# Two graph attention layers on one core: three PSUM banks for the lists' sums and a division one list later, one bank in turn for a closing's projections

## The chip, the cores and the metric

The kernel runs on one core of a Trainium2 chip. The metric is the device time of one execution in microseconds (us), from the runs shown below; lower is better. PE is the matmul engine, DVE the vector engine, ACT the scalar engine, POOL the general engine that issues the gathers here, and SP the engine that issues most other transfers. PE writes its results to PSUM[...]; DVE and ACT read them from there.

## The reference

Two layers over the same graph of 4096 nodes, whose adjacency is about 0.8% full and symmetric, with features of width 256. In each layer every node takes a softmax-weighted mean over its neighbours, adds its input and is normalised.

```python
def _gat(x, adj, W_heads, a1, a2, W_out, b_out):      # layer 0: 8 heads of 128
    Wh = jnp.einsum('nf,hfd->hnd', x, W_heads)
    s1 = jnp.einsum('hnd,hd->hn', Wh, a1)
    s2 = jnp.einsum('hnd,hd->hn', Wh, a2)
    e = s1[:, :, None] + s2[:, None, :]
    e = jnp.where(e > 0, e, ALPHA * e)
    e = jnp.where(adj[None, :, :] > 0, e, NEG)
    att = jax.nn.softmax(e, axis=-1)
    hp = jax.nn.elu(jnp.einsum('hnm,hmd->hnd', att, Wh))
    feat = jnp.transpose(hp, (1, 0, 2)).reshape(N, NHEADS * NHID)
    return feat @ W_out + b_out
...
x = _layernorm(x + _L0_gnn_ref(x, adj, ...), axis=-1)
x = _layernorm(x + _L1_gnn_ref(x, L1_gnn_W, L1_gnn_a, adj), axis=-1)   # layer 1: 4 heads of 64
```

## The kernel before

The two layers are done in different ways. The second is dense: all 4096 x 4096 weights are formed by DVE and multiplied by PE; it begins at about 1828 us of the profile, and the change touches none of it. The first is sparse, and everything that follows is about it.

**Lists.** The 4096 nodes are cut into 256 lists of 16 nodes (`T`), eight lists to a block of 128 nodes (`GT`), 32 lists to a phase (`GP`). For each list a selection on DVE has written the numbers of all neighbours outside the own block. POOL gathers the rows of these neighbours (features and score factors) into `G`, four gathers of 128 rows (L917), five lists ahead. DVE then forms the weights `e` of the list in `weigh` (a copy of the factors, three operations of 128x512 and a bit test; L1022 to L1037), for 8 heads times 16 nodes. `gathered` (L1040) sums rows times weights on PE in one PSUM bank, `po`: one matmul for the block's own rows (`own`), one for rows shared by four lists (`Gs`), four for `G`. Each fp32 matmul leaves two records in the profile, so a list has 12. Column 256 of `po` is the sum of the weights. `invert` (L1062) takes its reciprocal on DVE, `divide` (L1067) scales the sums on ACT into `ag`, which frees the bank, and `flip` (L1072) turns `ag` on PE (`pa`) and copies it on ACT into `aT`.

**The order.** Nothing reorders these instructions: each engine gets them in the order in which the loop at L1253 to L1321 writes them, and works them off in that order, waiting where it must. One pass of that loop (a turn, n) writes: the gathers of list n+5; `invert` and `divide` of list n - SOON; `flip` of list n - SOON - 1; `weigh` and `gathered` of list n; now and then the preparation of the next block's own rows (`Near`) and shared rows (`Shared`); a piece of counting the words for a later phase (`counts`, from turn 4 of a phase: a mask `mb` on ACT, two matmuls `pw` on PE, and twice a phase a copy `ws` on ACT, L613); some pieces of a later phase's selection on DVE (`pick`); and one piece of a closing (`late.some(1)`). SOON is 2.

**Closings.** When the eight lists of a block i are turned, `close0` (L1084) queues eight pieces, one for each of the next turns. They apply the head weights (`heads`, PE, L1105, in two halves of four heads, tiles `ph`), the ELU (`below` on ACT, L1115 and L1116, into `el`; `elu` on DVE, L1119, into `hT`) and the output projection (`project`, PE, L1126 and L1128, tile `py`). What needs the result comes with the pieces of the next closing, through the dictionary `st0["due"]`, ahead of that closing's own work in the same piece: `add` (DVE, L1134; reads `py`) in piece 0, and after every second block `spread`, `norm` and `flip` of two blocks (PE `pz`, ACT `x1T_sb`) in pieces 1 and 5 to 7.

```python
pieces = [
    [lambda: heads(0, 0)],
    [lambda: heads(0, 1)],
    [lambda: below(0), lambda: heads(1, 0)],
    [lambda: elu(0), lambda: heads(1, 1)],
    [lambda: below(1), lambda: project(0)],
    [lambda: elu(1), load],
    [lambda: project(1)],
    [],
]
```

**Second layer's scores.** When a quarter of the blocks is through (eight), `Scores.chunk` (L371) forms the second layer's scores for it in six steps (`scores` on PE into `ps`, `pull`, `top`, `factors`, `turn`, `store`), and `Projected.step` (L878) its projections; both go through `st0["then"]` and `st0["later"]` into the pieces of later closings. The same class forms the first layer's scores at the start (`opening`).

**PSUM.** Two banks serve all short transposes (`ps_m`), one holds DVE's small tables (`side`). Five belong to the pool `ps_0`: two with the tag `o0` for `po`, two with the tag `o1` for `ph`, `py` and `ps`, one with the tag `o2` for the words (`pw`, L600). A tile with one tag takes the tag's banks in turn, and its first writer waits until the last reader of what lay there is through.

Of the kernel before, what the change touches and what calls it, by code (L numbers as in the profile page):

```python
# [9 lines left out]
F32 = mybir.dt.float32  # L10
# [8 lines left out]
P = 128  # L19
# [243 lines left out]
def fast_path(  # L263
# [12 lines left out]
    N, F = x.shape  # L276
    D0, H0, _ = a0.shape
    D1, H1, _ = a1.shape
# [30 lines left out]
    ps_0 = first.enter_context(tc.tile_pool(name="ps_0", bufs=2, space=PSUM))  # L309
# [26 lines left out]
    class Scores:  # L336
# [29 lines left out]
        def chunk(self, k, src):  # L366

            n, H = self.n, self.H
            held = {}
            HC = CH // 2  # L370
            TH = HC // P  # L371

            def scores():
                ps = held["ps"] = ps_0.tile([P, HC], F32, tag="o1", name=f"ps_{n}_{k}")
                for c in range(KC):
                    for q in range(P // DQ):
                        a, half = divmod(q, 2)
                        nc.tensor.matmul(
                            ps[ts(q, DQ), :],
                            self.v[:, c, a, :],  # L380
                            src[:, c, ts(2 * k + half, HC)],
                            start=(c == 0),
                            stop=(c == KC - 1),
                            tile_position=(0, q * DQ),
                            skip_group_check=True,
                        )
# [652 lines left out]

    def gathered(n, G, e, own, shared):  # L1040

        po = ps_0.tile([P, F + 1], F32, tag="o0", name=f"po_0_{n}")

        def mul(w, v, first=False, **kw):
            nc.tensor.matmul(  # L1045
                po, w.rearrange("p h t -> p (h t)"), v[:, 0 : F + 1], start=first, **kw
            )

        mul(own.e[:, n % GT], own.rows, True, stop=False)
        a = ts(n % SL, SP)  # L1050
        mul(
            shared.e[a],
            shared.G[a],
            stop=False,
            tile_position=(n % SL * SP, 0),
            skip_group_check=True,
        )
        for b in range(NB):
            mul(e[:, b], G[:, b], stop=(b == NB - 1))
        return po  # L1060
# [21 lines left out]
    st0 = {}  # L1082

    def close0(i, aT):  # L1084


        hT = two.tile([P, H0, P], F32, tag="hT", name=f"hT_{i}", bufs=1)
        els, phs, pys = {}, {}, []
        if i % NY == 0:
            st0["mv"] = small.tile([P, NY, 2], F32, tag="mv0", name=f"mv0_{i}", bufs=2)  # L1090
            st0["rs"] = small.tile([P, NY], F32, tag="rs0", name=f"rs0_{i}", bufs=2)
            st0["ys"] = []
        mv, rs, ys = st0["mv"], st0["rs"], st0["ys"]

        def load():
            ys.append(two.tile([P, F], F32, tag="y", name=f"y_{i}", bufs=3))
            nc.sync.dma_start(ys[-1], x[ts(i, P), :])

        def heads(k, half):
            if half == 0:  # L1100
                phs[k] = ps_0.tile([P, 4, P], F32, tag="o1", name=f"ph_{i}_{k}")
            for hh in (2 * half, 2 * half + 1):
                h = 4 * k + hh
                for c in range(KC):
                    nc.tensor.matmul(  # L1105
                        phs[k][:, hh, :],
                        w_sb[:, c, ts(h, D0)],
                        aT[:, c, h, :],
                        start=(c == 0),
                        stop=(c == KC - 1),  # L1110
                    )

        def below(k):
            el = els[k] = two.tile([P, 4, P], F32, tag="el", name=f"el_{i}_{k}", bufs=1)
            nc.scalar.activation(el, phs[k], AF.Relu, scale=-1.0)  # L1115
            nc.scalar.activation(el, el, AF.Exp, scale=-1.0)  # L1116

        def elu(k):
            nc.vector.scalar_tensor_tensor(  # L1119
                hT[:, ts(k, 4), :], els[k], -1.0, phs[k], ALU.add, ALU.max  # L1120
            )

        def project(k):
            if k == 0:
                pys.append(ps_0.tile([P, F], F32, tag="o1", name=f"py_{i}"))
                nc.tensor.matmul(pys[0], ones[0:1, :], b_sb, start=True, stop=False)  # L1126
            for h in range(4 * k, 4 * k + 4):
                nc.tensor.matmul(  # L1128
                    pys[0], hT[:, h, :], wo_sb[:, h, :], start=False, stop=(h == H0 - 1)
                )  # L1130

        def add():
            y = ys[i % NY]
            nc.vector.tensor_tensor(y, y, pys[0], ALU.add)  # L1134
            st = small.tile([P, nc.vector.BN_STATS_DIM], F32, tag="st", name=f"st_0_{i}")
            nc.vector.bn_stats(st, y)
            nc.vector.bn_aggr(mv[:, i % NY, :], st)

        def spread():
            nc.vector.tensor_scalar(rs, mv[:, :, 1], EPS, None, ALU.add)  # L1140
            nc.gpsimd.tensor_tensor(rs, rs, neg_half.to_broadcast([P, NY]), ALU.pow)

        def norm(k):
            y = ys[k]
            nc.vector.tensor_scalar(
                y, y, mv[:, k, 0:1], rs[:, k : k + 1], ALU.subtract, ALU.mult
            )

        def flip(k):
            if not x1T:  # L1150
                x1T.append(big.tile([P, KC, N], F32, tag="xT", name="x1T_sb"))
            ii, y = i - NY + 1 + k, ys[k]
            nc.sync.dma_start(x1_d[ii], y)
            pz = ps_m.tile([P, KC, P], F32, tag="m", name=f"pz_{ii}")
            for cc in range(KC):
                nc.tensor.transpose(pz[:, cc, :], y[:, ts(cc, P)], ident)
            nc.scalar.copy(x1T[0][:, :, ts(ii, P)], pz)
            q = ii // CT
            turned[q] += 1
            if turned[q] == CT:  # L1160
                fs = sc1.chunk(q, x1T[0])
                m0 = q * CT
                steps = [lambda m=m: pair[0].step(m) for m in (m0, m0 + 4)]
                st0.setdefault("due", {}).setdefault(7, []).append(fs[0])
                st0["then"] = {k + 1: [f] for k, f in enumerate(fs[1:] + steps)}
                if q < NCH - 1:
                    st0["later"] = {
                        2 + k: [lambda m=m0 + 4 * k: pair[1].step(m, True)] for k in range(2)
                    }

        due = st0.pop("due", {})
        pieces = [
            [lambda: heads(0, 0)],
            [lambda: heads(0, 1)],
            [lambda: below(0), lambda: heads(1, 0)],
            [lambda: elu(0), lambda: heads(1, 1)],
            [lambda: below(1), lambda: project(0)],
            [lambda: elu(1), load],
            [lambda: project(1)],
            [],  # L1180
        ]
        for k, fs in due.items():
            pieces[k] = fs + pieces[k]
        late.add(*(lambda fs=fs: [f() for f in fs] for fs in pieces))
        due = st0["due"] = st0.pop("then", {})
        if "later" in st0 and due:
            st0["then"] = st0.pop("later")
        due.setdefault(0, []).append(add)
        if i % NY == NY - 1:
            for k, f in (  # L1190
                (1, spread),
                (5, lambda: norm(0)),
                (6, lambda: flip(0)),
                (6, lambda: norm(1)),
                (7, lambda: flip(1)),
            ):
                due.setdefault(k, []).append(f)
# [7 lines left out]
    pair = [Projected(g, wpool) for g in range(H1 // 2)]  # L1205
# [2 lines left out]

    NG = NT * GT
    AHEAD = 5  # L1210
    SOON = 2
    EXTRA = 2.5
    FIRST = 3.0
    COUNT = 4
# [23 lines left out]
    with tc.manual_schedule():  # L1238
# [13 lines left out]
        firsts.some(EARLY)  # L1252
        for n in range(NG + SOON + 1):  # L1253
            i, o, s = n // GT, n % GP, n // GP
            busy = 0.0
            if n < NG:
# [21 lines left out]
                if n % 4 == 2 and 2 <= n // 4 < 2 + NCH:  # L1278
                    inputs(1, n // 4 - 2)
            if SOON <= n < NG + SOON:  # L1280
                po, to = sums.pop(n - SOON)
                invert(n - SOON, po)
                means[n - SOON] = (divide(n - SOON, po), to)
            if n > SOON:
                ag, done = means.pop(n - SOON - 1)
                flip(n - SOON - 1, ag, done)
            if n < NG:
# [3 lines left out]
                m = n // SL + 1  # L1291
# [28 lines left out]
            if n > SOON and (n - SOON - 1) % GT == GT - 1:  # L1320
                close0((n - SOON - 1) // GT, done)  # L1321
    late.all()
    while "due" in st0 or "then" in st0:
        due = st0.pop("due", None) or st0.pop("then")
        for k in sorted(due):
            for f in due[k]:
                f()
# [186 lines left out]
    for g in range(G):  # L1514
        wh = pair[g].wh
        for c in range(NCH):
            po = open1(g, c)
# [8 lines left out]
            for j in range(NT):  # L1526
                if g + c == 0 and j % CT == CT - 2:
                    k = ts(j // CT, CT)
# [96 lines left out]
```

## Time and profile before

| | us |
|---|---|
| median of 3 runs | 2520.47 (2519.27 to 2523.54) |
| profiled execution, its own time | 2532.02 |
| its span, first to last instruction | 2530.2 |
| PE busy | 2133.9 |
| DVE busy | 1967.2 |
| ACT busy | 872.1 |
| POOL busy | 1083.4 |
| sums over lists, `G` rows (L1045), matmul busy | 623.4 (2048 records) |
| heads `ph` (L1105), matmul busy | 152.4 (1024 records) |
| projections `py` (L1128), matmul busy | 128.4 (512 records) |

The rows name a line, an engine, an operation and the tiles it writes and reads (out<-in). A wait of an engine is given with the instruction that waited, then `<-` and the instruction that ended the wait. "remote" (in the chain of waits: another core or an unknown queue) stands where the profile has no instruction for the semaphore that ended it; some matmul records are missing from the trace. The ends of matmuls are modelled. An fp32 matmul leaves two records, so 2048 records are 1024 matmuls.

### The profile page before, as it was taken

The numbers are of one execution on the slowest core, as the hardware profiler recorded it, in microseconds if no ns is written. First come the engines' busy times: TensorE is split into PE (matmuls) and PEld (weight loads), VectorE is DVE, ScalarE is ACT, GpSimd is POOL, SyncE is SP. The second block draws the span as 40 slices with busy tenths as digits, with TensorE's granted clock in tenths as the row PEclk, the third lists the DMA queues.
The fourth block names the chain that finished last, engine by engine and source line by source line (L and its number), as shares of the span: only waits on it lengthen the run. The fifth ranks groups of instructions, "written<-read, shape, count | busy, mean of one in ns | idle before, by whom it ended". The sixth has DMA issues, their size and how long they took to land.

```text
span 2530.2 us, 35637 instructions
## 1 busy us (share of the span) xinstructions
PE 2133.9 (84%) x12481; PEld 1217.2 (48%) x12481; DVE 1967.2 (78%) x4121; ACT 872.1 (34%) x1822; POOL 1083.4 (43%) x1154
## 2 busy tenths in 40 slices
PE   4377787888888887888887878878999999999997
PEld 2155455555556555555655655655643333333332
DVE  6478677787767878877786877666599999999997
ACT  1323323323323322332332222222344444455663
POOL 1455566566655666666566666656100000000000
PEclk9578888889878899888888889988999999999998
DMA  9777657456535746655564644444396666666763
GB/s 303 234 180 218 179 160 203 131 157 180 177 103 148 232 121 159 192 167 136 169 188 112 147 124 119 120 125 118 121 318 207 210 201 210 214 217 223 228 205 106
DMA packets 185796, 446.70 MB, mean 177 GB/s; under 512 B 60899, under 2 KB 92646, under 8 KB 185606
## 3 DMA queue, kind: packets, MB, share of 16 engines
q1 hardware_dynamic: 127462, 269.14, 33.8%
q0 software_dynamic: 52224, 169.97, 24.7%
q10 hardware_dynamic: 5920, 5.21, 0.6%
q8 instruction: 101, 1.65, 0.3%
q14 instruction: 89, 0.73, 0.1%
HBM read 427.62 MB, written 24.97 MB: 179 GB/s over the span
## 4 chain that ended last, share of the span: by engine, by line
PE 66%; another core or an unknown queue 13%; DVE 8%; ACT 7%; issue 4%; DMA 2%; POOL 0%; ACTq 0%; DVEq 0%; POOLq 0%; SPq 0%
PE po L1045 27%; PE po L1371 18%; PE po L1383 9%; PE py L1128 3%; PE ph L1105 3%; PE pa L1076 2%; ACT ag L1069 1%; ACT mb L588 1%; ACT rb_s L944 1%; PE pw L600 1%; DVE e L1023 1%; DVE e L1029 1%; PE pw L883 1%; DMA Ga<-in_adj 1%
## 5 line engine op out<-in xcount | busy, mean ns | idle before, releaser
L917 POOL DMA_INDIRECT G<-table,ids x1024 | 984.8, 962 | 610.9 <-issue 256.2
L1537 DVE SCALAR_TENSOR_TENSOR e<-rb,pj,mb 128x1024 f32<-128x1024 f32 x512 | 635.2, 1282 | 37.4 <-PE po L1383 13.3
L1045 PE MATMUL po<-G,e 128*128 128x257 f32 x2048 | 623.4, 456 | 17.8 <-DVE e L1037 7.7
L1371 PE MATMUL po<-e,wh 128*32 128x512 f32 x4096 | 531.3, 593 | 0.1
L1045 PEld LDWEIGHTS po<-G,e 128*128 128x128 f32 x2048 | 435.6, 224 | 186.3 <-issue 60.2
L1079 ACT COPY aT<-pa 128x256 f32<-128x256 f32 x256 | 95.3, 372 | 873.2 <-remote 267.0
L1045 PE MATMUL po<-own,eo 128*128 128x257 f32 x512 | 188.9, 454 | 237.6 <-ACT ag L1069 181.6
L1353 ACT ACTIVATE mb<-aq 128x1024 bf16<-128x1024 int32 x256 | 270.7, 1061 | 307.1 <-DVE e L1537 271.7
L1383 PE MATMUL po<-e,cj 128*32 128x512 f32 x2048 | 333.3, 592 | 0.0
L1371 PEld LDWEIGHTS po<-e,wh 128*32 128x32 f32 x4096 | 151.7, 110 | 289.7 <-issue 280.5
L1455 POOL TENSOR_SCALAR nm<-nm 128x4 f32<-128x4 f32 x6 | 5.5, 912 | 617.8 <-ACT ju L1454 617.8
L1064 DVE TENSOR_SCALAR rd_all<-po 128x1 f32<-128x1 f32 x256 | 38.7, 151 | 229.5 <-PE po L1045 153.0
L1045 PEld LDWEIGHTS po<-own,eo 128*128 128x128 f32 x512 | 86.9, 213 | 268.8 <-ACT ag L1069 202.4
L1045 PE MATMUL po<-Gs,e_s 32*128 32x257 f32 x512 | 202.7, 479 | 5.6 <-issue 5.6
L1023 DVE TENSOR_TENSOR e<-rb,side 128x512 f32<-128x512 f32 x256 | 176.0, 688 | 9.2 <-issue 0.2
L1029 DVE TENSOR_TENSOR e<-e,side 128x512 f32<-128x512 f32 x256 | 175.7, 686 | 8.8
L1037 DVE TENSOR_TENSOR e<-e,side 128x512 f32<-128x512 f32 x256 | 175.7, 686 | 8.8
L1105 PE MATMUL ph<-aT,w_sb 128*128 128x128 f32 x1024 | 152.4, 294 | 13.8 <-DVE hT L1119 6.7
L1383 PEld LDWEIGHTS po<-e,cj 128*32 128x32 f32 x2048 | 85.4, 110 | 149.0 <-issue 148.9
L1105 PEld LDWEIGHTS ph<-aT,w_sb 128*128 128x128 f32 x1024 | 140.7, 206 | 29.6 <-issue 16.5
L1069 ACT ACTIVATE ag<-po,rd_all 128x256 f32<-128x256 f32 x256 | 120.9, 472 | 70.4 <-DVE rd_all L1065 39.7
L1045 PEld LDWEIGHTS po<-Gs,e_s 32*128 32x128 f32 x512 | 84.7, 206 | 105.5 <-issue 105.4
(174 smaller groups left out, 2080.5 us busy)
## 6 DMA issues: line engine op xcount, KB each, us to landing
aq<-in_adjT SPq DMA_DIRECT2D x256, 512.0 KB
aq<-in_adj SPq DMA_DIRECT2D x108, 512.0 KB
rb<-r_d SPq DMA_DIRECT2D x48, 512.0 KB
G<-table,ids POOLq DMA_INDIRECT x1024
table<-in_x SPq DMA_DIRECT2D x8, 1024.0 KB
Ga<-in_adj SPq DMA_DIRECT2D x12, 512.0 KB
table<-tail SPq DMA_DIRECT2D x56, 98.0 KB
own<-table SPq DMA_DIRECT2D x32, 152.5 KB
```

Source lines behind the costliest of these rows:

```text
L917: nc.gpsimd.indirect_dma_start(out=G[:, b, :], out_offset=None, in_=table[s % 2][:, :], in_offset=bass.IndirectOffsetOnAxis(ap=lists[s][:, ...
L1023: nc.vector.tensor_tensor(e, rb[:, :, ts(n % GT, T)].unsqueeze(1).to_broadcast(sh), f_p[:, :, 0:H0].unsqueeze(3).to_broadcast(sh), ALU.mult,)
L1029: nc.vector.tensor_tensor(e, e, f_p[:, :, H0:].unsqueeze(3).to_broadcast(sh), ALU.max)
L1037: nc.vector.tensor_tensor(e, e, nb_p.unsqueeze(2).to_broadcast(sh), ALU.mult)
L1045: nc.tensor.matmul(po, w.rearrange("p h t -> p (h t)"), v[:, 0 : F + 1], start=first, **kw)
L1069: nc.scalar.activation(ag, po[:, 0:F], AF.Copy, scale=rd_all[:, n : n + 1])
L1079: nc.scalar.copy(aT[:, :, :, ts(n % GT, T)], pt)
L1105: nc.tensor.matmul(phs[k][:, hh, :], w_sb[:, c, ts(h, D0)], aT[:, c, h, :], start=(c == 0), stop=(c == KC - 1),)
L1353: nc.scalar.activation(mb, aq, AF.Relu, scale=OPEN)
L1371: nc.tensor.matmul(po[q][ts(b, DQ), :], wh[:, j, k, d : d + DQ], es[k][:, ts(q, HB)], start=(j == 0), stop=(j == NT - 1), tile_position=(0 ...
L1383: nc.tensor.matmul(po[NQ][r0 : r0 + DQ, :], sc1.cj[:, j, 2 * g + k : 2 * g + k + 1].to_broadcast([P, DQ]), es[k][:, ts(q, HB)], start=(j = ...
L1537: nc.vector.scalar_tensor_tensor(e, rb[k], sc1.pj[:, j, h : h + 1], mb, ALU.max, ALU.min)
```

## The change

The sums `po` get three banks (`o0`), and `SOON` becomes 3: list n - 3 is inverted and divided in turn n, list n - 4 is flipped. `ph` and `py` share one bank (`o1`), so that the halves of the heads and the projection of one closing lie there one after the other. The pieces of a closing are set anew: `heads(1, 0)` follows `elu(0)` in one piece, `project(0)` follows `elu(1)`, and the last piece, empty before, holds `project(1)`. The second layer's scores move to the words' bank (`o2`); the first layer's alternate between `o1` and `o2`. The steps of a quarter go through a list `st0["next"]` of two dictionaries: the six score steps in pieces 2 to 7 of one closing, the two or four projection steps in pieces 1 to 4 of the next.

```diff
--- before.py
+++ after.py
@@ -371,7 +371,10 @@
             TH = HC // P
 
             def scores():
-                ps = held["ps"] = ps_0.tile([P, HC], F32, tag="o1", name=f"ps_{n}_{k}")
+
+
+                tag = "o1" if n == 0 and k % 2 == 0 else "o2"
+                ps = held["ps"] = ps_0.tile([P, HC], F32, tag=tag, name=f"ps_{n}_{k}", bufs=1)
                 for c in range(KC):
                     for q in range(P // DQ):
                         a, half = divmod(q, 2)
@@ -1039,7 +1042,7 @@
 
     def gathered(n, G, e, own, shared):
 
-        po = ps_0.tile([P, F + 1], F32, tag="o0", name=f"po_0_{n}")
+        po = ps_0.tile([P, F + 1], F32, tag="o0", name=f"po_0_{n}", bufs=3)
 
         def mul(w, v, first=False, **kw):
             nc.tensor.matmul(
@@ -1098,7 +1101,7 @@
 
         def heads(k, half):
             if half == 0:
-                phs[k] = ps_0.tile([P, 4, P], F32, tag="o1", name=f"ph_{i}_{k}")
+                phs[k] = ps_0.tile([P, 4, P], F32, tag="o1", name=f"ph_{i}_{k}", bufs=1)
             for hh in (2 * half, 2 * half + 1):
                 h = 4 * k + hh
                 for c in range(KC):
@@ -1122,7 +1125,7 @@
 
         def project(k):
             if k == 0:
-                pys.append(ps_0.tile([P, F], F32, tag="o1", name=f"py_{i}"))
+                pys.append(ps_0.tile([P, F], F32, tag="o1", name=f"py_{i}", bufs=1))
                 nc.tensor.matmul(pys[0], ones[0:1, :], b_sb, start=True, stop=False)
             for h in range(4 * k, 4 * k + 4):
                 nc.tensor.matmul(
@@ -1161,30 +1164,29 @@
                 fs = sc1.chunk(q, x1T[0])
                 m0 = q * CT
                 steps = [lambda m=m: pair[0].step(m) for m in (m0, m0 + 4)]
-                st0.setdefault("due", {}).setdefault(7, []).append(fs[0])
-                st0["then"] = {k + 1: [f] for k, f in enumerate(fs[1:] + steps)}
+
                 if q < NCH - 1:
-                    st0["later"] = {
-                        2 + k: [lambda m=m0 + 4 * k: pair[1].step(m, True)] for k in range(2)
-                    }
+                    steps += [lambda m=m: pair[1].step(m, True) for m in (m0, m0 + 4)]
+                st0["next"] = [
+                    {k + 2: [f] for k, f in enumerate(fs)},
+                    {k + 1: [f] for k, f in enumerate(steps)},
+                ]
 
         due = st0.pop("due", {})
         pieces = [
             [lambda: heads(0, 0)],
             [lambda: heads(0, 1)],
-            [lambda: below(0), lambda: heads(1, 0)],
-            [lambda: elu(0), lambda: heads(1, 1)],
-            [lambda: below(1), lambda: project(0)],
-            [lambda: elu(1), load],
+            [lambda: below(0)],
+            [lambda: elu(0), lambda: heads(1, 0)],
+            [lambda: heads(1, 1)],
+            [lambda: below(1), load],
+            [lambda: elu(1), lambda: project(0)],
             [lambda: project(1)],
-            [],
         ]
         for k, fs in due.items():
             pieces[k] = fs + pieces[k]
         late.add(*(lambda fs=fs: [f() for f in fs] for fs in pieces))
-        due = st0["due"] = st0.pop("then", {})
-        if "later" in st0 and due:
-            st0["then"] = st0.pop("later")
+        due = st0["due"] = st0["next"].pop(0) if st0.get("next") else {}
         due.setdefault(0, []).append(add)
         if i % NY == NY - 1:
             for k, f in (
@@ -1208,7 +1210,7 @@
 
     NG = NT * GT
     AHEAD = 5
-    SOON = 2
+    SOON = 3
     EXTRA = 2.5
     FIRST = 3.0
     COUNT = 4
@@ -1320,8 +1322,7 @@
             if n > SOON and (n - SOON - 1) % GT == GT - 1:
                 close0((n - SOON - 1) // GT, done)
     late.all()
-    while "due" in st0 or "then" in st0:
-        due = st0.pop("due", None) or st0.pop("then")
+    for due in iter(lambda: st0.pop("due", None) or (st0.get("next") or [None]).pop(0), None):
         for k in sorted(due):
             for f in due[k]:
                 f()
```

## The prediction

> **What bounds the kernel now.** I read first the stage table (busy time in stretches), since 1,840 of the 2,530 us belong to the lists and the change touches nothing after them.
>
> ```profile
> core 0: us, PE busy (x) PEld busy (x) DVE busy (x) ACT busy (x) POOL busy (x), PEclk, DMA share, GB/s
> ...
> 800.00:1000.00 200.00, 164.59 (x727) 113.55 (x726) 155.31 (x419) 64.66 (x154) 127.45 (x133) 0.90 0.61 173
> ...
> 1840.00:2530.00 690.00, 672.14 (x6182) 218.20 (x6174) 641.21 (x568) 335.18 (x531) 18.27 (x26) 0.99 0.65 212
> ```
>
> In a stretch of lists PE has work for 82% and DVE for 78%: neither is full, so the time lies in waits. PE's own waits between 200 and 1800 us come next (total, times, longest), then DVE's and ACT's of the same stretch.
>
> ```profile
> PE po L1045 <- ACT ag L1069: 173.7, 63, 8.6
> PE po L1045 <- issue: 25.7, 28, 5.7
> PE po L1045 <- ACT lst L751: 13.6, 5, 5.6
> ...
> PE po L1045 <- DVE e L1037: 5.4, 7, 0.9
> ```
>
> ```profile
> DVE rd_all L1064 <- PE po L1045: 141.2, 70, 5.3
> DVE rd_all L1064 <- remote: 39.4, 18, 4.7
> ...
> DVE hT L1119 <- ACT el L1116: 31.8, 10, 7.1
> ```
>
> ```profile
> ACT aT L1079 <- remote: 257.8, 33, 12.4
> ACT aT L1079 <- PE pa L1076: 244.1, 68, 7.9
> ...
> ACT ag L1069 <- DVE rd_all L1065: 37.1, 22, 5.0
> ```
>
> At first sight this asks for the change: PE waits 173.7 us for `ag`, the division that frees a bank of sums, and almost never (5.4 us) for the weights `e`. DVE stands 181 us before its inverse, for PE. But who keeps `ag` waiting? The timeline of one such wait answers:
>
> ```profile
> 1067.04 0.27 PE L1076 MATMUL pa<-ident,ag 128*128 128x128 f32 x1 [0.26 <-issue]
> ...
> 1070.63 0.37 ACT L1079 COPY aT<-pa 128x256 f32<-128x256 f32 x1 [8.69 <-remote]
> ...
> 1070.90 1.15 ACT L588 ACTIVATE mb<-aq,half 128x1024 bf16<-128x1024 int32 x1
> ...
> 1071.95 0.68 ACT L613 ACTIVATE ws<-pw,half 128x512 f32<-128x512 f32 x1
> ...
> 1072.53 0.47 ACT L1069 ACTIVATE ag<-po,rd_all 128x256 f32<-128x256 f32 x1
> ...
> 1073.05 1.23 PE L1045 MATMUL po<-own,eo 128*128 128x257 f32 x2 [5.75 <-ACT ag L1069]
> ```
>
> ACT stands 8.69 us before the copy of a transposed mean, which waits for PE; then copy, mask, words and `ag` follow without a gap, and PE starts 0.05 us after `ag`. DVE's inverse was not what `ag` waited for. I followed all PE gaps ahead of `own` from list 8 on in this way (230 us in all), back along ACT's unbroken run to the instruction that had been idle. About 11 us (16 gaps) begin with `ag` itself waiting for DVE. About 200 us begin with ACT waiting for something of PE (copies of `pa`, `pz`, `pmg`, `pf`, `pw`), in some 45 cases several us after the profile shows PE done.
>
> **What the Trainium skill says.** "TensorE: Matmul & The Clock Gate", section "Architectural detail: the array is 16× 32×32, not 1× 128×128", says that ACT and DVE take their queues strictly in order; the fence above shows just that. The same page, "What's actually happening", has PE at half clock after an idle window of about 3.4 us; the trace agrees (a list's 12 matmul records take 3.26 us, after a long gap 6.10 us). "Perfetto Trace Analysis", section "Optimization Strategy", reads repeated bubbles as a possible lack of PSUM: here the bank is what PE waits for, but not what is missing. The same page, "Tensor Engine Instruction (MATMUL, LD_WEIGHTS)", says ends of matmuls are estimates; that fits ACT seeing `pa` 3.3 us after its shown end (1067.31 to 1070.63).
>
> **The change, part by part.**
>
> *Third bank, division three lists behind.* `divide(n - SOON)` is issued in turn n, and list n takes the bank that this same division frees. Before, n waits for `ag` of n-2, after for `ag` of n-3, but both stand at the same place of ACT's queue: behind everything of turn n-1, the `aT` copy above all, and that copy waits for PE's transposes of turn n-1. So the loop PE, ACT, PE stays one turn long. What goes is `ag` waiting for DVE: about -11 us on PE's path, at most the 48 us (37.1 + 11.3) that ACT stood there. DVE may be one list further ahead, so the weights come earlier: the fourth wait of PE above is 5.4 us, all gaps ahead of `po<-G,e` 17.8 us; I take -6, bounds 0 and -18. DVE's 181 us are idle time of an engine that PE hardly waits for, and count as nothing.
>
> *One bank in turn for a closing.* No instruction is added: PE, DVE, ACT and POOL have the same ones, SP splits one merged run of stores differently. But three PE steps of each closing now need a DVE step of the same turn: heads 0 after `add` of the closing before, heads 1 after `elu(0)`, the projection after `elu(1)`. Behind each on PE stand the next transposes and list, and ACT and DVE wait for these. The cover is that DVE is ahead. Over the timeline I compared, for the turns where these now fall (n mod 8 = 4, 7, 2), when DVE was done with its turn and when PE was done with its list: DVE is earlier by 3.9, 3.1 and 4.5 us in the median. With the DVE step added (0.41 and 0.69 us) the cases in which DVE is late add up to 0.4 + 12.8 + 1.5 = 15 us, of which 12.5 in two turns. I take +15. If DVE were never ahead, each of 32 closings would show twice 0.60 + 0.63 + 0.69 + about 0.1 = 2.0 us, 130 us: the upper bound. If always ahead, 0.
>
> *`add` one turn behind its projection (was two).* DVE waits for PE's last projection and PE's heads wait for DVE, so a late completion hits here as well. About 45 such stretches in 256 lists make 6 of 32 closings; what they lose is that the heads (8 records, 1.06 us, double at half clock) come after the wait and not during it. An estimate of +8, bounds 0 and +12.
>
> *Pieces moved.* `flip(1)` now shares its turn with two us of projection (8 records, 1.99), which covers the copy `x1T`; such gaps that begin at an ordinary `pz` or `pa` were 7 us: -5. Against it, the turns of `below` have no PE work of their own any more; there ACT needs 0.47 + 0.37 + 1.15 + 1.24 = 3.2 us and PE's list with its transposes 3.7, so nothing is exposed at full clock: 0. The four projection steps of a quarter in a row put 1.75 us of ACT work each under 1.95 us of PE: 0. SP issues the same loads, a turn or so later; POOL's `rs` waits behind gathers four turns ahead of its use: 0. Second-layer scores in the words' bank: by the order they come in turn 30 of a phase and are read by turn 1 of the next, while words are counted from turn 7 to 22: 0. The opening's scores alternate over two banks as before: 0.
>
> *The end.* After the last list nothing covers the closing:
>
> ```profile
> 1808.81 0.60 ACT L1115 ACTIVATE el<-ph 128x512 f32<-128x512 f32 x1 [1.93 <-PE ph L1105]
> 1809.43 0.63 ACT L1116 ACTIVATE el<-el 128x512 f32<-128x512 f32 x1
> 1810.10 0.69 DVE L1119 SCALAR_TENSOR_TENSOR hT<-el,ph 128x512 f32<-128x512 f32 x1 [2.98 <-ACT el L1116]
> ...
> 1810.84 0.69 PE L1126 MATMUL py<-b_sb,ones 1*128 1x256 f32 x2 [0.34 <-DVE hT L1119]
> ```
>
> The second half's heads run under `el` now; after, they wait for 1810.8, take 2.1 us, and `el` and `elu` of the second half (2.0 us) then stand open too before the projection: +4. One more turn of draining: +1.
>
> Sum: -11 - 6 + 15 + 8 - 5 + 5 = +6 us. The profiled execution took 2532.0 us (span 2530.2 and 1.8 around it), 11.5 above the median of the runs, 2520.5; all terms are differences, so 2538 there and 2526.5 here.
>
> **Rivals.**
> *Faster: DVE's lead pays.* If the long stalls end sooner because DVE and PE have a list more between them, a third of the 173.7 us goes: -58, 2462 us. For it: 181 us of DVE waits vanish, and `e` is ready in most of PE's gaps. Against it: ACT's run without a gap ahead of `ag`. It decides where ACT idles directly ahead of `ag`; there only some 10 us do.
> *Much slower: the single bank is a chain.* If DVE loses its lead (through `add`, which now ties it to PE's previous turn), a quarter of the 130 us shows, +33 and 2560 with the rest of the sum. For it: DVE already waits 31.8 us for `el`. Against: the medians of 3 to 4 us. It decides where DVE ends its turn after PE's list.
> *Nothing moves.* Lockstep of bank and division leaves all waits as they are, DVE's lead stays, the end alone counts: +5, 2525 us.
>
> **How the numbers follow.** A measurement of this kernel tells about 0.2% (5 us) from no change. My forecast's own range is -5 to +25 us, chance 0.50: slower 0.30, same 0.18, faster 0.02. Much slower 0.18. Nothing moves 0.08: same 0.06, slower 0.02. Faster 0.24, of which 0.01 stays within 0.2%. Together: slower 0.50, same 0.25, faster 0.25. Range: leaving out the 0.10 of the faster case below 2496 and 0.08 of the slower above 2562.
>
> **What would show it.** Right: PE's wait for `ag` stays above 130 us in 200 to 1800; DVE's wait at its inverse falls well below 100 us; new PE waits `ph` or `py` for DVE `y` and `hT`, 5 to 40 us together; the last closing about 4 us longer; the second layer's 690 us unchanged. Wrong: `ag` waits below 80 us and a list stage shorter by 30 us or more, or PE's waits for `hT` and `y` over 60 us.

## The result and the profile after

| | before | after |
|---|---|---|
| median, us (20 runs each, on one chip) | 2523.86 (2512.5 to 2540.47) | 2524.04 (2499.4 to 2541.59) |
| ratio after to before, 95% interval | | 0.9986 (0.9963 to 1.0009) |
| profiled execution: span, us | 2530.2 | 2527.0 |
| lists 7 to 255 (first `G` matmul of list 7 to last of list 255), us | 1638.2 | 1626.9 |
| from there to the last closing's heads | 6.1 | 10.0 |
| last closing's heads to the end of its `add` | 9.0 | 13.0 |
| from there to the first weights of the second layer | 11.7 | 12.2 |
| second layer, to the end | 702.9 | 702.6 |

No difference that can be measured: the interval reaches from 9 us faster to 2 us slower. Ratios, here and below, are estimated from fast executions alone; one of the 20 after was slow. The five lower rows are read off the two timelines; one profile of each stands behind them, and single executions of one kernel differ by 40 us, so the 11 us of the lists say nothing by themselves. The 8 us at the end are another matter, since a chain of instructions shows them: at full clock the last closing takes 13.0 us again in the profiles of runs 1 and 5 below, and 9.0 in runs 7 and 8, which keep the closings of before.

The stage table after:

```profile
core 0: us, PE busy (x) PEld busy (x) DVE busy (x) ACT busy (x) POOL busy (x), PEclk, DMA share, GB/s
800.00:1000.00 200.00, 169.73 (x749) 117.03 (x748) 154.47 (x421) 63.57 (x155) 125.34 (x130) 0.90 0.59 166
1840.00:2530.00 690.00, 668.87 (x6154) 219.25 (x6143) 638.02 (x566) 333.48 (x530) 17.11 (x26) 0.99 0.65 210
```

The list stage has PE at 85% and DVE at 77%: still nobody is full. PE's waits between 200 and 1800 us, then DVE's, then ACT's (total, times, longest, in us):

```profile
PE po L1048 <- ACT ag L1072: 155.8, 63, 11.2
PE po L1048 <- issue: 38.7, 31, 4.4
...
PE po L1048 <- DVE e L1040: 8.8, 12, 1.1
```

```profile
DVE hT L1122 <- ACT el L1119: 74.1, 22, 11.9
DVE y L1137 <- PE po L1048: 59.0, 9, 12.2
DVE y L1137 <- PE py L1131: 42.7, 7, 8.1
...
DVE y L1137 <- remote: 27.3, 5, 8.9
DVE y L1137 <- PE pa L1079: 21.5, 6, 6.7
...
DVE rd_all L1067 <- PE po L1048: 7.7, 3, 4.6
```

```profile
ACT ag L1072 <- DVE rd_all L1068: 50.9, 29, 3.6
```

PE's wait for `ag` is there as before, 63 times in both. DVE's wait at its inverse is gone (7.7 us), but DVE did not come free: about the same time now stands ahead of `add` (`y`, 160 us with all that ended it; 17 before) and ahead of `elu` (`hT`, 74.1 us for `el`; 31.8 before). And ACT waits for DVE's inverse no less than before, 50.9 us where it was 37.1.

One wait for `ag`, followed in the timeline of the changed kernel (start, duration):

```profile
1006.33 0.38 PE L1079 MATMUL pa<-ident,ag 128*128 128x128 f32 x2
...
1007.71 2.00 PE L1048 MATMUL po<-G,e 128*128 128x257 f32 x8
...
1017.43 0.37 ACT L1082 COPY aT<-pa 128x256 f32<-128x256 f32 x1 [12.02 <-remote]
...
1017.70 1.21 ACT L947 COPY rb_s<-rb 32x128 f32<-32x128 f32 x4
...
1018.94 1.15 ACT L591 ACTIVATE mb<-aq,half 128x1024 bf16<-128x1024 int32 x1
...
1019.99 0.46 ACT L1072 ACTIVATE ag<-po,rd_all 128x256 f32<-128x256 f32 x1
...
1020.50 0.80 PE L1048 MATMUL po<-own,eo 128*128 128x257 f32 x1 [7.10 <-ACT ag L1072]
```

It is the picture of before: ACT idle ahead of `aT`, then its run (copy, four `rb_s`, mask), `ag`, and PE 0.05 us after it. The transposes that the copy at 1017.43 reads are those of 1006.33, because the next copy, behind `ag`, belongs to the next turn. PE had gone on with a whole list by then, and only the news of it came late, over ten microseconds after the shown end. While PE then stood, the granted clock fell to half at 1014.7, 3.4 us after PE's last closely spaced work; in another such wait of this trace it fell at 966.9, 5.0 us after it. The Trainium skill, "TensorE: Matmul & The Clock Gate", section "What's actually happening", puts the fall after an idle window of about 3.4 us; what the traces show of it stands at the end.

### The profile page after: what moved, and what is told of

The parts are those of the page before. It is cut to its first block, busy times and chain, and to the rows that moved or that the text cites. A ratio compares the mean times of both kernels' runs of the same rounds, so it can differ in the third digit from the quotient of the medians.

```text
span 2527.0 us, 35628 instructions
## 1 busy us (share of the span) xinstructions
PE 2126.7 (84%) x12481; PEld 1210.1 (48%) x12481; DVE 1962.4 (78%) x4121; ACT 874.4 (35%) x1822; POOL 1081.4 (43%) x1154
## 4 chain that ended last, share of the span: by engine, by line
PE 62%; DVE 14%; another core or an unknown queue 10%; ACT 6%; issue 5%; DMA 3%; POOL 1%; DVEq 0%; ACTq 0%; POOLq 0%; SPq 0%
PE po L1048 24%; PE po L1372 18%; PE po L1384 9%; PE py L1131 3%; PE ph L1108 2%; DVE e L1026 2%; DVE e L1032 2%; PE pa L1079 2%; DVE e L1040 1%; ACT ag L1072 1%; ACT mb L591 1%; PE pw L886 1%; DMA Ga<-in_adj 1%; PE pw L603 1%
## 5 line engine op out<-in xcount | busy, mean ns | idle before, releaser
L1108 PE MATMUL ph<-aT,w_sb 128*128 128x128 f32 x1024 | 152.5, 293 | 20.4 <-issue 15.3
L1137 DVE TENSOR_TENSOR y<-y,py 128x256 f32<-128x256 f32 x32 | 13.5, 421 | 164.4 <-PE po L1048 59.0
```

The source lines that it names most:

```text
L1108: nc.tensor.matmul(phs[k][:, hh, :], w_sb[:, c, ts(h, D0)], aT[:, c, h, :], start=(c == 0), stop=(c == KC - 1),)
```

## The experiments

Three chips were used, one for each group of four; each ratio is against the kernel before on the same chip. The chips differ in how late PE's results reach ACT, and where they come promptly the kernel before takes 12% less time, more than any edit changed:

| chip | runs | kernel before, us | from the shown end of the transposes `pa` to the start of their copy `aT` (lists 32 to 255) |
|---|---|---|---|
| first | 1 to 4 | 2530.6 (14 runs) | division early: median 2.83 us, 88 of 224 over 4 us, longest 13.2 |
| second | 5 to 8 | 2224.1 (22 runs) | both heads in one piece: median 0.04 us, none over 4 us, longest 3.7 |
| third | 9 to 12 | 2521.4 (59 runs) | changed kernel: median 1.50 us, 54 over 4 us, longest 12.0 |

The two traces compared above are of the late kind (before: median 1.77, 62 over 4 us; after: 1.19, 47 over 4 us). "Late chip" and "prompt chip" below mean this. In other things the chips are alike: the second layer takes 703 us in the trace of before and 704 in run 5, a gather 964 and 958 ns, a DVE step of 128x512 686 ns in both. The difference lies in the lists (1638 and 1361 us).

**1. The bank freed a turn earlier.**

```diff
-    SOON = 3
+    SOON = 2          # on the changed kernel: three banks stay
```

> The changed kernel with the division two lists behind again (SOON 2) and everything else kept, three banks for the sums included: list n then takes the bank that was divided in turn n-1, a full turn earlier. Lockstep theory (a third bank gains nothing as long as the division is put off with it): PE's wait for ag between 200 and 1800 us falls from 155.8 us to below 80, DVE's wait at its inverse comes back (from 7.7 to above 100 us), and the time is 20 to 80 us below the changed kernel. Rival, PE's stalls are its own (its results are handed on late, whatever bank it has): ag waits fall, but PE then waits for e or for its transposes by the same amount, and the time is within 10 us of the changed kernel. Rival, DVE's lead is what the third list buys: losing it costs, the time is 10 to 40 us above the changed kernel.

Measured: 2474.96 us, 0.9782 of the kernel before (0.9744 to 0.982). PE's and DVE's waits between 200 and 1800 us:

```profile
PE po L1048 <- issue: 59.9, 73, 2.9
PE po L1048 <- DVE e L1040: 40.5, 29, 3.6
...
PE po L1048 <- DVE side L1034: 20.4, 8, 4.7
```

```profile
DVE rd_all L1067 <- remote: 51.8, 18, 6.6
...
DVE rd_all L1067 <- PE po L1048: 34.9, 23, 3.8
```

`ag` is gone from PE's list. All gaps of PE ahead of `own` in lists 32 to 255 came to 203 us before the change, 182 after it, and 4 here. The results were late here too (first row of the table above), so they did not become prompter; PE had another bank to go on with. About 50 us come back as waits of PE for the weights and their tables (40.5 and 20.4 here, 8.8 and 3.6 after the change). DVE waits at its inverse again, and that is not free: followed back along DVE's unbroken run, some 26 us of these waits begin there. The changed kernel was not timed on this chip; the gain is against the kernel before. This is the lockstep theory's case: the third bank was worth nothing as long as the division was put off with it. The rival in which PE's own stall is the cost falls, and so does the one in which the third list of lead is what gains.

**2. The closing's single bank alone.** (Also run 12.)

```diff
-    SOON = 3
+    SOON = 2
-        po = ps_0.tile([P, F + 1], F32, tag="o0", name=f"po_0_{n}", bufs=3)
+        po = ps_0.tile([P, F + 1], F32, tag="o0", name=f"po_0_{n}")
```

> Division two lists behind and two banks for the sums, as before the change; only the closing's single bank with its pieces set anew, and the scores in the words' bank. By the terms of the prediction (single bank +15, add one turn behind its projection +8, pieces moved -5, end +4) it is 22 us slower than the kernel before, and PE's waits ph and py for DVE come to 15 to 40 us in 200 to 1800. If the single bank is hidden altogether, it is within 5 us of the kernel before, but for 4 us at the end. If the single bank is a chain, it is 35 us slower or more. The difference between the changed kernel and this one is what the third bank with the later division is worth: -17 us by the prediction, 0 if nothing moves, -40 or more if DVE's lead pays.

Measured: 2554.93 us, 1.0099 (1.0066 to 1.0131), 24 us over the kernel before, which is the prediction's 22 in size. The waits do not bear it out: between 200 and 1800 us PE waited for DVE's `hT` and `y` at `ph` and `py` 4.1 us in all, where 15 to 40 were expected. But the profile is of the fastest of the nine executions (2535.3 us), 5 us over the kernel before, and can't show where the median's 24 us lie. Run 12 on the third chip then showed no loss at all. What holds on this first chip is the pair of runs 2 and 1, which differ in the bank alone: 2555 to 2475 us.

**3. `add` two turns behind its projection.**

```diff
-            [lambda: heads(0, 0)],
-            [lambda: heads(0, 1)],
+            [],
+            [lambda: heads(0, 0), lambda: heads(0, 1)],
...
-        due.setdefault(0, []).append(add)
+        due.setdefault(1, []).append(add)
```

> The changed kernel with add of a closing moved from piece 0 to piece 1 and both halves of heads 0 behind it in the same piece, so that add is two turns behind its projection as before the change. By the prediction add one turn behind its projection costs 8 us (0 to 12): this kernel is 0 to 12 us faster than the changed kernel, and DVE's wait ahead of y (about 160 us of idle time with all its enders) falls below 80. If DVE's waits cost PE nothing, DVE's wait falls just the same and the time is within 3 us of the changed kernel. If four PE steps of heads in one turn hurt more than the wait did, it is slower by up to 10 us.

Measured: 2562.03 us, 1.0115 (1.007 to 1.016). DVE's wait ahead of `y` fell to about 19 us as expected, but the kernel got slower, not faster; DVE's wait ahead of `hT` rose to 144 us. The changed kernel itself was not timed on this chip other than in run 4's one execution (2542 us, with its end shortened), so how much of the 1.15% is this edit's stays open. DVE's 160 us ahead of `y` were not time to be won here: most of them went, and no gain came.

**4. The last closing on two banks.**

```diff
-                phs[k] = ps_0.tile([P, 4, P], F32, tag="o1", name=f"ph_{i}_{k}", bufs=1)
+                last = i == NT - 1 and k == 1
+                phs[k] = ps_0.tile([P, 4, P], F32, tag="o0" if last else "o1",
+                                   name=f"ph_{i}_{k}", bufs=3 if last else 1)
...
+        if i == NT - 1:
+            pieces = [
+                [lambda: heads(0, 0), lambda: heads(0, 1)],
+                [lambda: heads(1, 0), lambda: heads(1, 1)],
+                [lambda: below(0)], [lambda: elu(0)],
+                [lambda: below(1), load], [lambda: project(0)],
+                [lambda: elu(1)], [lambda: project(1)],
+            ]
```

> The changed kernel, but the last closing alone takes a bank of the sums (free by then) for the second half of its heads, and has the order of the pieces that the kernel before had. By the prediction the single bank costs 4 us there: from the start of the last closing's heads to the end of its add it took 8.6 us before the change and takes 12.6 us after; here 8.6 again. If the end's length comes from elsewhere (the three turns of draining), it stays near 12.6. The whole span can't tell 4 us; the timeline of the end can.

One execution, 2542.17 us. First the end of the changed kernel, then that of this one:

```profile
1799.18 2.02 PE L1108 MATMUL ph<-aT,w_sb 128*128 128x128 f32 x16 [0.60 <-DVE y L1137]
...
1803.27 2.05 PE L1108 MATMUL ph<-aT,w_sb 128*128 128x128 f32 x16 [2.07 <-DVE hT L1122]
...
1807.39 0.69 PE L1129 MATMUL py<-b_sb,ones 1*128 1x256 f32 x2 [2.07 <-DVE hT L1122]
...
1811.77 0.42 DVE L1137 TENSOR_TENSOR y<-y,py 128x256 f32<-128x256 f32 x1 [4.44 <-PE py L1131]
```

```profile
1815.64 3.85 PE L1115 MATMUL ph<-aT,w_sb 128*128 128x128 f32 x32
...
1820.44 0.69 PE L1136 MATMUL py<-b_sb,ones 1*128 1x256 f32 x2 [0.95 <-DVE hT L1129]
...
1824.82 0.42 DVE L1144 TENSOR_TENSOR y<-y,py 128x256 f32<-128x256 f32 x1 [2.37 <-PE py L1138]
```

From heads to the end of `add` it is 9.6 us here (and in runs 6 and 11), 13.0 after the change, 9.0 before it; the 8.6 and 12.6 of the expectation end where `add` starts. So 3.4 of the 4.0 us were the single bank with the order that it asks for. The stretch ahead of the heads stayed long (10.9 us; 6.1 before), so that part is not the last closing's own. It comes with the single bank and the new pieces of the closings ahead of it, which no run takes apart.

**5. Both halves of heads 0 in one piece, `add` where it was.** (Also run 10.)

```diff
-            [lambda: heads(0, 0)],
-            [lambda: heads(0, 1)],
+            [],
+            [lambda: heads(0, 0), lambda: heads(0, 1)],
```

> The changed kernel with both halves of heads 0 in piece 1, while add stays in piece 0, one turn behind its projection. It takes apart what the run with add one piece later mixed: there DVE's wait for the projection was gone, and yet the kernel was 1.15% slower than before the change. Cover theory (in lockstep, PE's closing work in a turn hides ACT's run up to the next ag; a turn with four copies rb_s that loses its heads shows that run): as slow as that run, 20 to 40 us over the changed kernel, with PE's gaps ahead of own in turns 4 and 5 of eight near 30 us each (changed kernel 14 and 11), although DVE's wait ahead of y stays above 60 us. Rival, the place of add made the loss (DVE held back at turn 4 does some good): then this kernel is within 8 us of the changed kernel.

Measured on the prompt chip: 2256.38 us, 1.0153 (1.0126 to 1.018). The changed kernel was not run there, so this decides nothing between the two theories, and how much of the 1.5% belongs to the change itself stays open too; run 10 repeats the comparison on a chip where both were timed. The chip itself was the news.

**6. The two edits together** (runs 1 and 4; also run 11).

> The two edits that helped, together: division two lists behind with three banks (2475 us against 2531 us of the kernel before on that chip, ratio 0.978), and the second bank for the last closing's heads (3.4 us shorter there). If they add up, 0.976 to 0.978 of the kernel before. If the end hides behind the loads of the second layer's masks and scores, 0.978 to 0.980.

Measured on the prompt chip: 2217.24 us, 0.9969 (0.9961 to 0.9978). Against the kernel before that is a gain of 7 us, an eighth of run 1's 56, and outside the expected range. PE's waits between 200 and 1500 us of run 5 (division three behind), and of this run with its stage from 800 to 1000 us:

```profile
PE po L1048 <- ACT ag L1072: 76.5, 61, 3.8
PE po L1048 <- DVE e L1040: 44.5, 63, 1.8
```

```profile
PE po L1048 <- DVE e L1040: 104.1, 88, 3.7
PE py L1136 <- DVE hT L1129: 9.3, 13, 1.4
```

```profile
800.00:1000.00 200.00, 179.51 (x856) 125.76 (x856) 187.66 (x514) 75.00 (x170) 151.57 (x160) 0.97 0.74 205
```

With prompt results PE waits for `ag` half as long to begin with, and what an earlier bank takes away there (76.5 us) comes back for the larger part as waiting for `e`: DVE, busy for 187.7 of the 200 us, is close to full.

But the kernel before is not the only comparison. Run 6 is 39 us (1.7%) faster than run 5, with the lists at 1336 us instead of 1361. The two also differ in the end (3.4 us) and in the place of heads 0, so this is not the bank's worth alone; but the earlier bank may be worth more than 0.3% here, if the closing's single bank costs time on this chip. No run on it tells the two apart. What keeps `ag` waiting is also not the same: of run 5's 81.5 us of PE gaps ahead of `own` from list 8 on, none begins with ACT waiting for the transposes, and 33 begin with `ag` waiting for DVE's inverse.

**7 and 8. The third bank alone, and its control.** In both, DVE's tables (`side`, cut to the columns in use) move from PSUM to SBUF; run 7 then has `bufs=3` for `po` on the kernel before, run 8 has not.

```diff
-    ps_f = first.enter_context(tc.tile_pool(name="ps_f", bufs=1, space=PSUM))
+    ps_f = first.enter_context(tc.tile_pool(name="ps_f", bufs=1))
...
-        po = ps_0.tile([P, F + 1], F32, tag="o0", name=f"po_0_{n}")
+        po = ps_0.tile([P, F + 1], F32, tag="o0", name=f"po_0_{n}", bufs=3)
```

> The kernel before with DVE's small tables in SBUF instead of PSUM, and the bank that this sets free given to the sums: three banks, division two lists behind, closings on two banks in their old order. To be read against the kernel with the tables in SBUF alone. Lockstep theory: a third bank with the division unmoved takes the waits for ag away as it did with the closing on one bank (from 2555 to 2475 us, -3.1%): here -2 to -4%, PE's wait for ag below 60 us. If the closing's single bank had been what made room for that gain, less than -1%.

> Control for the run with the third bank alone: the kernel before with DVE's small tables in SBUF and nothing else changed. Nothing in the traces so far shows DVE with these operands in SBUF. If an operand's place is indifferent, within 0.3% of the kernel before; if DVE's five steps of a list become slower by more than PE's slack, slower by 1 to 10%, and the comparison with a third bank then says less about PE's wait.

Measured: 2349.37 us, 1.0561 (1.0544 to 1.0579), and 2349.15 us, 1.0564 (1.0549 to 1.0579). The bank took PE's 52 us for `ag` away, and the time did not move, where -2 to -4% was expected: with the tables moved DVE waits about 170 us for gathered rows in both runs, and this on the prompt chip. As a test of lockstep the pair is inconclusive. What the tables did is told at the end.

**9 to 12. Four kernels on one late chip.** The changed kernel, runs 5, 6 and 2 once more.

> The changed kernel once more, beside the three that follow, on one chip. The kernel before took 2224 us on the chip of the last runs and 2531 us on that of the first, and PE's results came late on the second only (no stretch of over 2 us with several of PE's semaphore updates in a bunch on the first, 40 to 61 such stretches in each profile on the other). If this chip holds results back: 0.996 to 1.001 of the kernel before, as in the first comparison. If it doesn't, DVE is close to the bound (187.7 of 200 us busy with the early bank), the third bank has little to win, and the single bank's waits decide: 1.000 to 1.012.

> The changed kernel with both halves of heads 0 in piece 1, add still in piece 0: now against the changed kernel on the same chip (on another chip it was 1.53% slower than the kernel before, and the changed kernel had not been run there). Cover theory: 0.6 to 1.8% slower than the changed kernel. Rival, the place of add made the loss of the run with add moved: within 0.3% of it.

> Division two lists behind with three banks, and the last closing on two banks. On a chip that holds PE's results back: 0.974 to 0.980 of the kernel before. On one that doesn't: 0.996 to 0.998, as measured on such a chip. The gain of an earlier bank is that of riding out late results.

> The closing's single bank with its pieces, division two behind, two banks for the sums. On a chip that holds PE's results back, 1.007 to 1.013 of the kernel before, as in the first run of it, and the changed kernel 20 to 35 us below it. On one that doesn't, the waits of PE and DVE within a turn are still there, but with PE never late they cost less: 1.003 to 1.012, and the changed kernel within 10 us of it.

| run | us | ratio to before, 95% interval |
|---|---|---|
| 9, changed kernel | 2518.85 | 0.9993 (0.9972 to 1.0013) |
| 10, both heads in one piece | 2524.59 | 1.0001 (0.9978 to 1.0024) |
| 11, division early, end on two banks | 2449.02 | 0.9714 (0.9682 to 0.9745) |
| 12, single bank alone | 2520.47 | 1.0000 (0.9981 to 1.0019) |

Run 10: the cover theory falls on this chip. Which of the two turns holds heads 0 makes no difference that shows. Run 11: the version that beats both kernels, 2.9% below the kernel before (a little more than expected) and 2.8% below the changed one. Run 12: the single bank with its pieces costs nothing here, where run 2 had it at 1%; the expectation missed. PE's waits there between 200 and 1800 us are these:

```profile
PE po L1048 <- ACT ag L1072: 169.2, 63, 10.8
PE ph L1108 <- DVE hT L1122: 7.9, 5, 3.0
PE py L1129 <- DVE hT L1122: 3.5, 2, 2.1
```

That is about where the kernel before stood (173.7 us for `ag`, and already 6.7 us for `hT` at `ph`). Runs 9 and 12 differ in the third bank with the later division alone: 0.9993 against 1.0000, each known to about 0.2%, so some 2 us of gain, give or take 7.

## Why the prediction was right, and where only its sum was

The time was right (2526.5 forecast, 2524.0 measured), and the reasoning on lockstep was right and is shown on late chips. That the two times lie so close is luck: several terms of the sum were too large, each in its direction, and cancelled. The rival "nothing moves" (2525 us) describes what happened better than the forecast's own parts do.

- *Lockstep of bank and division.* Right. PE's wait for `ag` stayed at 155.8 us (above 130 was forecast), and freeing the bank a turn before its use, run 1, took it to nothing and 2 to 3% off the kernel on late chips.
- *"What goes is `ag` waiting for DVE: about -11 us."* This step failed. That wait rose, from 37.1 + 11.3 to 50.9 + 15.4 us. It had risen already with the single bank alone (70 and 72 us in runs 2 and 12), and the later division did not bring it down again (77 us in run 9; one profile each). The later inverse is ready earlier only if DVE gets to it earlier, and DVE is now held a few instructions up in the same queue, at `add` and `elu`, with 160 and 74 us of idle time. I had taken DVE's wait at its inverse to be simply gone; it moved to the single bank's readers. The -6 us for `e` failed alike (5.4 us before, 8.8 after). Together -17 was forecast, and runs 9 and 12 show -2, give or take 7.
- *Single bank +15, `add` one turn behind +8, pieces -5.* Mis-sized in sum: +18 without the end, +22 with its 4. Run 12 has 0, give or take 5; run 2 has +24 on another chip of the late kind. The direct waits of PE at `ph` and `py` for `y` and `hT` were 5.7 us after the change, the lower edge of the forecast's 5 to 40, and the kernel before had 6.7 already. On the third chip DVE's lead, on which I had counted turn by turn, bears a step more without PE noticing. Why the first chip shows a loss stays open, and so does what the single bank costs on the prompt chip.
- *Steps taken at zero* (projection steps in a row, scores in the words' bank, second layer). No wait of the changed kernel names them among its larger ones; the second layer took 702.6 us against 702.9.
- *The end, +4 +1.* The +4 was exact at full clock: 13.0 us against 9.0. But of the eight profiles with this ending only three kept full clock (after, runs 1 and 5). In runs 2, 3, 9, 10 and 12 the granted clock fell to half in the new gaps, and the last closing took 16.0 to 16.9 us; run 9 is the changed kernel itself. So the term is +4 to +8, and this term of the forecast left the clock out. The draining was +3.9 (+7.2 in run 9) and not +1: the two closings that are still under way after the last list now wait for `hT` and `y` in turn (1.45 and 0.60 us on PE) and have nothing beside them. Run 12 shows the same with the division two behind (10.5 us), so it belongs to the single bank and its pieces, not to the later division.
- *The Trainium skill's reading of bubbles.* I had set aside "Perfetto Trace Analysis", section "Optimization Strategy" (repeated bubbles may mean too little PSUM), with the words that the bank is what PE waits for, but not what is missing. That was too strong. A bank more was missing, as run 1 shows; what the change did was to add it and in the same step to keep it occupied one list longer.
- *The late copies.* The prediction took ACT's 3.3 us after the shown end of `pa` as a sign that shown ends are estimates. On the prompt chip the same step is 0.04 us in the median, so the shown ends are close, and the 3.3 us are a result that came late.
- *Much slower rival* (2560 us). With +33 in place of +15 the rest of the sum gives 2544.5; 2560 comes out only if the two gains (-11 and -6) go as well.
- *Faster rival* ("DVE's lead pays", -58). Its size was there to be had, but not by DVE's lead: run 1 gives the lead back and is 56 us below the kernel before.

## What to carry to other kernels

A buffer more pays only for the turns by which it comes free ahead of its use: if the step that frees it is put off by as many turns as buffers are added, the loop between the engines keeps its length. What the turns are worth depends on how late results come, so compare on one chip. Find the instruction that frees the buffer and what stands ahead of it in its engine's queue, and compare turn numbers, before counting buffers. When a wait of an in-order engine vanishes from one instruction, look for it at the instructions just ahead in the same queue before booking it as gained.

## What the runs showed of the hardware that was not expected

**Results of PE that come late, on some chips.** On two chips (and in the traces of before and after) ACT sees the end of PE's transposes 1.0 to 2.8 us after the shown end in the median and up to 13 us after it; on the second chip 0.04 us and at most 3.7. PE meanwhile goes on with the next list. In the trace's record of PE's semaphore updates (the signals by which PE tells others that it is done) these are pauses that end with a bunch of updates; their lengths pile up at 2.1, 2.8, 4.3, 5.7, 7.1, 8.5 and 9.9 us. Counting pauses of over 2 us that end with at least four updates within 0.6 us, the profiles of late chips have 34 to 61 each, 200 to 350 us in sum, none of them in the second layer; the four of the prompt chip have none. The kernel before took 2224 us there and 2521 to 2531 us elsewhere. That the lateness makes this difference is likely, since the lists alone differ, but no run switches it off. Its cause is not known: the pauses meet instruction fetches no more often than chance would have it (9 of 43 before, 15 by chance), the gathers had landed, and all executions here were recorded ones, so none shows whether recording plays a part. The records of late chips are incomplete too (about 2,000 of PE's 2,326 updates are in them, all on the prompt chip), so the counts are rough; that ACT waits is not in doubt.

On late chips this also says what the earlier bank buys: slack to ride out such a pause. With the closing's single bank and its pieces it came to 2.2 and 2.9% of the kernel before there, and to 0.3% on the prompt chip. The bank alone is worth 3.1% on the first chip (runs 2 and 1); on the prompt chip its own worth was not measured.

**A clock that follows how full PE was.** In each trace the granted clock (PEclk in the views) is 1.00 or 0.50 and changes only at multiples of 3.413 us from its first change. Cut into these stretches, the lists (200 to 1450 us of all 14 traces) show 577 falls to half clock. Each came after a stretch in which PE was busy for at most 0.70 of the time (median 0.37), and a stretch below 0.41 was always followed by one. The 580 returns to full clock each came after a stretch at 0.77 or more. The ends of matmuls are modelled, so the shares are rough. No idle window is needed, then, and here the measurement goes against the page named above. In the last closing of run 9 PE never stands longer than 2.1 us, but in the second stretch below it is busy for only 1.34 of 3.41 us, and the clock falls at its end:

```profile
core 0: us, PE busy (x) PEld busy (x) DVE busy (x) ACT busy (x) POOL busy (x), PEclk, DMA share, GB/s
...
1788.02:1791.44 3.42, 2.81 (x21) 2.39 (x19) 1.03 (x3) 0.00 (x0) 0.00 (x0) 1.00 0.00 0
1791.44:1794.85 3.41, 1.34 (x12) 1.15 (x11) 0.69 (x1) 1.23 (x2) 0.00 (x0) 1.00 0.00 0
1794.85:1798.26 3.41, 1.71 (x9) 1.42 (x7) 0.37 (x1) 1.23 (x2) 0.00 (x0) 0.50 0.00 0
```

The last projection (`py`) then, first in the profile of the changed kernel that kept full clock, and in run 9:

```profile
1808.01 3.72 PE L1131 MATMUL py<-wo_sb,hT 128*128 128x256 f32 x16
```

```profile
1799.78 6.33 PE L1131 MATMUL py<-wo_sb,hT 128*128 128x256 f32 x16
```

So a chain that makes PE wait for DVE and ACT in turn can cost more than its waits.

**Tables in SBUF slow the gathers.** The groups of POOL's gathers, between 200 and 1500 us, with DVE's tables in PSUM (run 6) and in SBUF (run 8):

```profile
L920 POOL DMA_INDIRECT G<-table,ids x942 | 901.0, 956 | 288.5 <-issue 218.1 <-PE po L1048 23.2 <-DVE side L1034 7.0
```

```profile
L916 POOL DMA_INDIRECT G<-table,ids x871 | 947.7, 1088 | 263.9 <-issue 192.1 <-PE po L1044 28.5 <-DVE side L1030 12.2
```

A gather takes 1088 ns instead of 956. Run 6 differs from run 8 in more than the tables, but the kernel before, which differs in the tables alone, has 964 on its chip, and run 7 has 1087. DVE's own five steps are hardly slower (696 ns against 687 for the first of 128x512), but DVE then stands 170.8 us for gathered rows that were not there, and the kernel loses 5.6%. The Trainium skill, "SBUF — State Buffer", section "Who interferes with whom", has a DVE instruction with two SBUF inputs contend with a POOL instruction that reads SBUF. That fits: with the tables there, four of DVE's five steps have both inputs in SBUF, and a gather reads its list of row numbers. The runs show the slowdown, not its path.
